# A graph network's second pass: twelve products done during the neighbour search, rows weighed in batches, norm products on four row groups

## The chip, the cores and the metric

The kernel runs on one core of one Trainium2 chip. The metric is device time in microseconds of one execution; the number compared is the median of several. Engines: PE (TensorE; PEld is its weight load), DVE (VectorE), ACT (ScalarE), POOL (GpSimd), SP (SyncE, which issues most DMAs).

## The reference, cut to what matters

Four graph layers over 2708 nodes with 128 features and a dense 2708 x 2708 matrix `adj`. The change lies in layer 0:

```python
def _lap_mul(A, x):
    d = 1.0 / jnp.sqrt(jnp.sum(A, axis=-1))
    return d[:, None] * (A @ (d[:, None] * x))
z = _lap_mul(A, x) @ W1 + b1
z = jax.nn.leaky_relu(z, negative_slope=0.1)
sq = jnp.sum(z * z, axis=-1)
d2 = jnp.maximum(sq[:, None] + sq[None, :] - 2.0 * (z @ z.T), 0.0)
S = jnp.exp(-jnp.sqrt(d2 + 1e-10) / 2.0)
S = jnp.where(ranks < 4, S, 0.0)        # the four nearest rows alone
A2 = S + A
out = _lap_mul(A2, x) @ W2 + b2
x = _layernorm(x + out)
```

Layers 1 to 3 (an attention layer and two more products with `adj`) follow; their code is the same before and after.

## The kernel before, in words

The nodes are 22 tiles of 128 rows, `t` = 0 to 21; the last has 20 rows (`FULL` = 21). The columns are C = 6 chunks of 512, 512, 512, 512, 384 and 276. `adj` is used transposed. Its row tiles 0 to 15 (`S` = 16) are streamed as panels of four tiles by one chunk (1 MB for a chunk of 512) through a ring of four slots; tiles 16 to 21 lie in SBUF for good (`res`).

**First pass** (lines 425 to 540): `adj` times y, then z for each tile, its transpose `zT`, and the norms. `turn_norms` writes `nsq3`, 3 rows of bf16 parts of the negated norms, on partitions 0 to 2.

**Search** (lines 623 to 651): for each tile, in the order 4 to 15, 0 to 3, 16 to 21 (n counts them from 0): ACT makes `z2` = 2 z (line 626); PE does six norm products `ones3` by `nsq3` (line 632, three rows deep, bf16) and six products `z2` by `zT` (line 642, f32) into the same six banks; ACT copies the six banks into one of three `key` buffers (line 643); DVE takes the eight largest (`max`, line 644, into `near`) and where they stand (`max_index`, line 645, into `where`).

**Weighing** (`weigh`, lines 586 to 617): for a range of tiles, the values in `near` become the weights `sim` of the four nearest, the new degrees `d2inv`, and the scaled rows `y2` = x times d2inv, which POOL multiplies and stores to DRAM (`y2_rows`); `others` sets a tile's own row apart. It is called three times: tiles 0 to 16 after t = 16, tiles 17 to 19 after t = 19, and 20, 21 at the end. The small arithmetic is DVE's, with Ln and Exp on ACT.

**Second pass** (`by_panels` at line 869): `adj` times `y2`, chunk by chunk, 22 products a chunk into one bank (acc pool of three). The 20-row products of three chunks go together, on three groups of 32 rows (`few`, line 96). Chunk 0 takes its tiles in the order 0 to 11, 16 to 19, 12 to 15, 20, 21. `ready` are the four panels of chunk 0, loaded before the search.

**Work hung on ticks** (`Due`, line 31): in the second pass PE, DVE and ACT run in the order written. Each product is a tick (132 in all), and `at(n, f)` puts work f behind tick n. `sum_near(t)`, at tick `near_at[t]` = 24 + 4.6 t, gathers three near rows of y2 for each row of the tile (POOL, line 672) and adds them up on DVE (line 685). `end_pass2(c)` sets out a chunk's end: `finish` (add_near on PE, the copy into hT on ACT, line 832) at n, no earlier than three ticks behind its last sum_near and 16 behind the chunk before; then norm0 at n + 2, turn at n + 9, find_c at n + 11, and for its tiles compare (DVE), times_w (PE, ACT), rank_rows (ACT) and rank_columns (PE) from n + 13 on. The last chunk's steps stand closer together (lines 851 to 866). `due.flush` runs what is left after the last product.

**PSUM** has eight banks: in the search six for `acc` and two for `mis`; in the pass three and three, one for `rk` and one for the places (`js_pool`, used after the pass).

Of the kernel before, what the change touches and what calls it, by code (L numbers as in the profile page):

```python
# [13 lines left out]
ALU = mybir.AluOpType  # L14
# [16 lines left out]
class Due:  # L31


    def __init__(self):
        self.n, self.work = 0, []

    def at(self, n, f, *args):
        self.work.append((n, len(self.work), f, args))
        self.work.sort(key=lambda w: w[:2])
# [13 lines left out]
def kernel(  # L53
# [54 lines left out]
    mis_pool = psum.enter_context(tc.tile_pool(name="mis", bufs=2, space=bass.MemoryType.PSUM))  # L108
# [80 lines left out]
    def by_panels(weights, done, tick=None, ready=(), first=None):  # L189

        ready = list(ready)
        accs = {}

        def product(c, i, src, w):
            lhsT = weights(i)[few(c) if i == FULL else slice(None)]
            start = c not in accs  # L200
            if start:
                accs[c] = acc_tile()
            stop = tick is None and i == (FULL if c % GROUPS == 0 else FULL - 1)
            nc.tensor.matmul(accs[c][: lhsT.shape[-1], :w], lhsT=lhsT, rhs=src, start=start, stop=stop)  # L204

        for c in range(C):
            w = cw[c]
            for i in [*(first if first and c == 0 else range(FULL)), *([FULL] if c % GROUPS == 0 else [])]:
                if i == FULL:
                    for n in range(c, c + GROUPS):  # L210
                        product(n, i, res[few(n), i - S, cols[n]], cw[n])
                    done(c, accs[c])
                    for _ in range(GROUPS if tick is not None else 0):
                        tick()
                    continue
                if i < S:
                    if i % 4 == 0:
                        if ready:
                            part = ready.pop(0)
                        else:  # L220
                            part = load_panel(i // 4, c)
                    src = part[:, i % 4, :w]
                else:
                    src = res[:, i - S, cols[c]]
                product(c, i, src, w)
                if i == FULL - 1 and c % GROUPS:
                    done(c, accs[c])
                if tick is not None:
                    tick()

# [133 lines left out]
    with tc.tile_pool(name="knn", bufs=1) as knn:  # L364
        nsq = knn.tile([P, T], F32, tag="nsq", name="nsq")
        nsq3 = knn.tile([3, N], BF16, tag="nsq3", name="nsq3")
        ones3 = knn.tile([3, P], BF16, tag="ones3", name="ones3")
# [47 lines left out]
        def turn_norms(c, ts, parts):  # L415
            ps = mis_tile()
            for t in ts:
                o = t * P - starts[c]
                nc.tensor.transpose(ps[:3, o : o + pw[t]], parts[: pw[t], t - ts[0], :], ident[: pw[t], : pw[t]])
            nc.scalar.copy(nsq3[:, cols[c]], ps[:3, : cw[c]])  # L420
# [165 lines left out]
        def weigh(ts):  # L586
# [4 lines left out]
            nc.vector.tensor_add(nr, nr, nsq[:, t0:t1, None].to_broadcast([P, t1 - t0, TOPK]))  # L591
            nc.vector.tensor_scalar(nr, nr, 0.0, DIST_EPS, op0=ALU.min, op1=ALU.subtract)
# [4 lines left out]
            nc.vector.tensor_reduce(dd, sm, AX.X, ALU.add)  # L597
            nc.vector.tensor_add(dd, dd, deg[:, t0:t1])  # L598
# [20 lines left out]
        ready = [load_panel(g, 0) for g in range(G)]  # L619
        tc.keep_in_program_order(nc.scalar.preload_act_table_set("natural_log_exp_and_others"))  # L620
        with tc.tile_pool(name="keys", bufs=3) as keys:

            for n, t in enumerate([*range(4, S), *range(4), *range(S, T)]):
                p = pw[t]
# [5 lines left out]
                def norms(c):  # L630
                    cs = cols[c]
                    nc.tensor.matmul(pks[c][:p, : cw[c]], lhsT=ones3[:, :p], rhs=nsq3[:, cs], start=True, stop=False)
# [5 lines left out]
                for c in range(C) if n else (5, 3, 2, 4, 1, 0):  # L638
                    if not n:
                        norms(c)  # L640
                    cs = cols[c]
                    nc.tensor.matmul(pks[c][:p, : cw[c]], lhsT=z2[:, :p], rhs=zT[:, cs], start=False, stop=True)  # L642
                    nc.scalar.copy(key[:p, cs], pks[c][:p, : cw[c]])  # L643
                nc.vector.max(near[:p, t, :], key[:p])  # L644
                nc.vector.max_index(where[:p, t, :], near[:p, t, :], key[:p])
                if t == T - 6:
                    weigh(range(0, T - 5))
                if t == T - 3:
                    weigh(range(T - 5, T - 2))
            weigh(range(T - 2, T))  # L650
# [5 lines left out]
    js_pool = psum.enter_context(tc.tile_pool(name="places", bufs=1, space=bass.MemoryType.PSUM))  # L656
# [161 lines left out]
    near_at = [24 + (23 * t) // 5 for t in range(T)]  # L818
# [49 lines left out]
    with tc.manual_schedule(engines={nc.tensor.engine, nc.vector.engine, nc.scalar.engine}):  # L868
        by_panels(
            rows_of(y2), end_pass2, due.tick, ready, [*range(S - 4), *range(S, T - 2), *range(S - 4, S), T - 2]  # L870
        )
        due.flush()
    late.close()
    more = ExitStack()
# [744 lines left out]
```

## Time and profile before

| | us |
|---|---|
| five runs | 1095.9, 1098.95, 1093.81, 1090.37, 1093.31 |
| their median | 1093.81 |
| the profiled execution: its time | 1099.03 |
| the profiled execution: its span | 1097.3 |
| mean granted PE clock in it | 0.966 |
| PE busy in the span | 999.9 (91%) |
| DVE / ACT / POOL busy | 643.0 / 338.9 / 266.2 |

Times in the trace count from the span's start. The first pass ends at about 157 us, the search runs to 302, the second pass from 295 to 443, the ranking to about 540, the attention layer's blocks to 760, and two more passes and the last layer to the end. A line of a timeline gives the start, the length, the engine, the source line, the operation, out<-in, and how many were merged; what stands in brackets is the idle time before it and what ended that. A matmul of f32 shows as two records.

### The profile page before, as it was taken

The page shows a single profiled execution, that of the slowest core. Times are in us where ns is not written, and L with a number is a line of the kernel's source. Part 1 is how long each engine was busy: PE and PEld are TensorE (multiplying, and loading weights), DVE is VectorE, ACT ScalarE, POOL GpSimd, SP SyncE. Part 2 cuts the span into 40 slices and gives each one's busy share as a digit, 9 for nine tenths or more (in the row PEclk, how much of TensorE's full clock was granted, in tenths as well). Part 3 has the DMA queues.
Part 4 walks back from the last instruction along what each step waited for, and adds up shares of the span by engine and source line. Part 5 has one row for each costly group of instructions (what it writes and reads, how often), then busy time and mean ns, then how long its engine had stood idle before and what let it go on. Part 6 is the DMA issues. An engine that isn't in the chain of part 4 may idle for free.

```text
span 1097.3 us, 11424 instructions
## 1 busy us (share of the span) xinstructions
PE 999.9 (91%) x3678; PEld 482.3 (44%) x3678; DVE 643.0 (59%) x1351; ACT 338.9 (31%) x614; POOL 266.2 (24%) x332
## 2 busy tenths in 40 slices
PE   0798999999995988698799999999999999999996
PEld 0345544444442556443233333334444644564444
DVE  5884448999942658763398999998112112132122
ACT  0000125555400234602466777665001100011000
POOL 4000000000564554106485444441112100000000
PEclk9989999999997999699899999999999999999998
DMA  9999330000283747398445545555674865574752
GB/s 341 362 320 276 115 120 1 0 1 1 61 283 92 229 133 215 131 326 267 126 131 160 143 134 152 148 150 188 208 252 140 280 223 187 172 238 156 243 159 75
DMA packets 109363, 190.30 MB, mean 173 GB/s; under 512 B 13650, under 2 KB 46690, under 8 KB 109294
## 3 DMA queue, kind: packets, MB, share of 16 engines
q1 hardware_dynamic: 91408, 151.79, 42.7%
q0 software_dynamic: 17712, 37.62, 12.4%
q8 instruction: 31, 0.51, 0.2%
q14 instruction: 38, 0.31, 0.1%
q10 hardware_dynamic: 174, 0.08, 0.0%
HBM read 214.37 MB, written 4.16 MB: 199 GB/s over the span
## 4 chain that ended last, share of the span: by engine, by line
PE 47%; DMA 1%; issue 1%; DVE 1%; POOL 0%; ACT 0%; SPq 0%; POOLq 0%; DVEq 0%
PE acc L204 27%; PE hacc L1280 9%; PE num L1423 9%; PE mis L285 1%; DMA ring<-in_adjT,slot_i 0%; PE mis L1554 0%; DMA ring<-carry 0%; ACT gb L234 0%; PE mis L1520 0%; PE mis L1550 0%; POOL ring L1301 0%; SPq L1438 0%; POOL rstd L253 0%; PE mis L1508 0%; POOL xws L890 0%
## 5 line engine op out<-in xcount | busy, mean ns | idle before, releaser
L1301 POOL DMA_INDIRECT ring<-in_adjT,slot_i x88 | 99.0, 1125 | 115.1 <-PE num L1423 88.0
L1423 PE MATMUL num<-ring,lw 128*64 128x512 f32 (+1 forms) x528 | 116.1, 561 | 3.1 <-DVE err L1265 1.3
L1280 PE MATMUL hacc<-inv,xws 128*128 128x512 f32 (+1 forms) x264 | 111.7, 559 | 0.4 <-issue 0.4
L642 PE MATMUL acc<-zT,z 128*128 128x512 f32 (+4 forms) x264 | 108.6, 558 | 0.0
L1255 ACT ACTIVATE inv<-num,plain 128x1024 f32<-128x1024 f32 x88 | 80.5, 915 | 61.4 <-PE num L1423 53.1
L253 POOL TENSOR_TENSOR rstd<-rstd,minus_half 128x4 f32<-128x4 f32 (+1 forms) x19 | 18.2, 956 | 315.0 <-DVE rstd L252 315.0
L643 ACT COPY key<-acc 128x512 f32<-128x512 f32 (+3 forms) x132 | 70.1, 534 | 59.9 <-issue 29.8
L234 ACT COPY gb<-acc 128x512 f32<-128x512 f32 (+2 forms) x18 | 9.6, 534 | 251.1 <-PE acc L204 251.1
L1265 DVE TENSOR_TENSOR err<-inv,num 128x1024 f32<-128x1024 f32 x88 | 74.3, 853 | 20.3 <-ACT inv L1258 18.6
L204 PE MATMUL acc<-ring,y 128*128 128x512 f32 (+2 forms) x192 | 81.1, 551 | 0.5 <-POOL sim L579 0.5
L1280 PEld LDWEIGHTS hacc<-inv,xws 128*128 128x128 f32 x264 | 46.5, 189 | 77.4 <-issue 48.1
L672 POOL DMA_INDIRECT got<-y_rows,where x66 | 69.8, 1058 | 43.1 <-DVE near_sum L685 22.7
L204 PE MATMUL acc<-ring,xs 128*128 128x512 f32 (+2 forms) x192 | 77.9, 549 | 0.0
L1272 DVE SCALAR_TENSOR_TENSOR inv<-gb,g_inv,inv 128x1024 f32<-128x1024 f32 x88 | 77.0, 912 | 0.1
L204 PE MATMUL acc<-ring,carry 128*128 128x512 f32 (+2 forms) x192 | 74.5, 542 | 0.0
L204 PE MATMUL acc<-ring,m_rows 128*128 128x512 f32 (+2 forms) x192 | 74.3, 542 | 0.0
L1269 DVE SCALAR_TENSOR_TENSOR inv<-err,inv 128x1024 f32<-128x1024 f32 x88 | 72.6, 863 | 0.1
L642 PEld LDWEIGHTS acc<-zT,z 128*128 128x128 f32 (+1 forms) x264 | 47.5, 188 | 55.0 <-issue 49.6
L1258 ACT ACTIVATE inv<-inv 128x1024 f32<-128x1024 f32 x88 | 67.6, 768 | 2.8
L644 DVE MAX8 near<-key 128x8 f32<-128x2708 f32 (+1 forms) x22 | 65.5, 2979 | 4.9 <-ACT key L643 4.9
L570 POOL TENSOR_TENSOR slot_e<-near,sim 128x44 f32<-128x44 f32 (+2 forms) x3 | 0.7, 241 | 271.8 <-DVE d2inv L598 267.7
L1423 PEld LDWEIGHTS num<-ring,lw 128*64 128x64 f32 x528 | 37.1, 139 | 64.4 <-issue 45.6
(327 smaller groups left out, 1376.6 us busy)
## 6 DMA issues: line engine op xcount, KB each, us to landing
ring<-in_adjT SPq DMA_DIRECT2D x86, 1024.0 KB
ring<-in_adjT SPq DMA_DIRECT2D x19, 768.0 KB
part<-in_adjT SPq DMA_DIRECT2D x12, 1024.0 KB
ring<-in_adjT SPq DMA_DIRECT2D x19, 552.0 KB
res<-in_adjT SPq DMA_DIRECT2D x4, 1280.0 KB
more<-in_adjT SPq DMA_DIRECT2D x4, 1024.0 KB
part<-in_adjT SPq DMA_DIRECT2D x3, 768.0 KB
part<-in_adjT SPq DMA_DIRECT2D x3, 552.0 KB
```

Of the source, the lines that this page charges most:

```text
L204: nc.tensor.matmul(accs[c][: lhsT.shape[-1], :w], lhsT=lhsT, rhs=src, start=start, stop=stop)
L642: nc.tensor.matmul(pks[c][:p, : cw[c]], lhsT=z2[:, :p], rhs=zT[:, cs], start=False, stop=True)
L643: nc.scalar.copy(key[:p, cs], pks[c][:p, : cw[c]])
L672: nc.gpsimd.indirect_dma_start(out=got[:p, :], out_offset=None, in_=y2_rows[:, :], in_offset=bass.IndirectOffsetOnAxis(ap=where[:p, t, k : ...
L1255: nc.scalar.activation(inv, num[:, :w], AF.Ln, scale=plain[:, 0:1], bias=plain[:, 1:2])
L1258: nc.scalar.activation(inv, inv, AF.Exp, scale=-1.0)
L1265: nc.vector.tensor_mul(err, inv, num[:, :w])
L1269: nc.vector.scalar_tensor_tensor(inv, err, 2.0, inv, op0=ALU.subtract, op1=ALU.mult)
L1272: nc.vector.scalar_tensor_tensor(inv, gb[:, col : col + w], g_inv[:, q : q + 1], inv, op0=ALU.max, op1=ALU.mult)
L1280: nc.tensor.matmul(haccs[:, o:e], lhsT=xws[:, q, :], rhs=inv[:, o:e], start=(q == 0), stop=(q == NQ - 1))
L1301: nc.gpsimd.indirect_dma_start(out=rows[i][:KC, n, :], out_offset=None, in_=adj_half[:, :], in_offset=bass.IndirectOffsetOnAxis(ap=slot_i[ ...
L1423: nc.tensor.matmul(num[n * (BJ + 2) : (n + 1) * (BJ + 2), o:e], lhsT=lw[:, 2 * q + n, :], rhs=rows[i][:, n, c0 + o : c0 + e], start=True, ...
```

## The change

It does these things:

- The last norms in hand, three DMAs on SP copy the rows 0 to 2 of `nsq3` to partitions 32, 64 and 96 (`NORMS` = 4). From the second tile of the search on, the norm product of chunk c reads row group c % 4. `ones3` and `nsq3` are made that tall.
- The two `mis` banks are given back before the search, and one bank, `acc0`, is taken for chunk 0 of the second pass.
- The four panels of chunk 0 are loaded behind those copies, in the order 1, 2, 3, 0. From the seventh to the eighteenth tile of the search (n = 6 to 17) PE also does the product of chunk 0 with tile n - 2 (4 to 15) into `acc0`. When a panel's fourth product has been put in, the first, second and third panel of chunk 1 are loaded in its place.
- PE's order in the search is the order written, from the second tile on.
- `weigh` is called for tiles 4 to 7, 8 to 11, 12 to 15 and 0 to 3, each after the last tile of the four, with its arithmetic on POOL (the sum over four weights as four additions); then for 16 to 19 after t = 19 and for 20, 21 at the end, on DVE as before.
- The second pass begins with chunk 0's tiles 0 to 3 and 16 to 19, then chunk 1's 0 to 3, then chunk 0's 20 and the 20-row products, then the rest of chunk 1; the other chunks as before. That makes 120 ticks. `near_at[t]` = 23 + 4.2 t. `by_panels` takes the order and the bank begun as arguments.
- The places' bank is taken after the pass, when `acc0` has been given back. `Due` numbers its entries by a counter of all that were put in (before, by the length of the list at that time).

```diff
-    def by_panels(weights, done, tick=None, ready=(), first=None):
+    def by_panels(weights, done, tick=None, ready=(), order=None, begun=None):
...
-        accs = {}
+        accs = dict(begun or {})
+        started = set(accs)
...
+        if order is None:
+            order = [(c, i) for c in range(C) for i in [*range(FULL), *([FULL] if c % GROUPS == 0 else [])]]
+        for c, i in order:
...
-            nc.scalar.copy(nsq3[:, cols[c]], ps[:3, : cw[c]])
+            nc.scalar.copy(nsq3[:3, cols[c]], ps[:3, : cw[c]])
...
-        def weigh(ts):
+        def weigh(ts, engine):
...
-            nc.vector.tensor_add(nr, nr, nsq[:, t0:t1, None].to_broadcast([P, t1 - t0, TOPK]))
-            nc.vector.tensor_scalar(nr, nr, 0.0, DIST_EPS, op0=ALU.min, op1=ALU.subtract)
+            engine.tensor_add(nr, nr, nsq[:, t0:t1, None].to_broadcast([P, t1 - t0, TOPK]))
+            engine.tensor_scalar(nr, nr, 0.0, DIST_EPS, op0=ALU.min, op1=ALU.subtract)
...
-            nc.vector.tensor_reduce(dd, sm, AX.X, ALU.add)
-            nc.vector.tensor_add(dd, dd, deg[:, t0:t1])
+            if engine is nc.vector:
+                nc.vector.tensor_reduce(dd, sm, AX.X, ALU.add)
+                nc.vector.tensor_add(dd, dd, deg[:, t0:t1])
+            else:
+                engine.tensor_add(dd, sm[:, :, 0], deg[:, t0:t1])
+                for k in range(1, TOPK):
+                    engine.tensor_add(dd, dd, sm[:, :, k])
...
-        ready = [load_panel(g, 0) for g in range(G)]
+        mis_psum.close()
...
+        acc0 = first_pool.tile([P, CW], F32, tag="first", name="acc0")
+        for g in range(1, NORMS):
+            nc.sync.dma_start(nsq3[32 * g : 32 * g + 3, :], nsq3[:3, :])
+        AHEAD = range(4, S)
+        panels0 = {g: load_panel(g, 0) for g in (*range(1, G), 0)}
+        ready = [panels0[0]]
+        batches = {7: range(4, 8), 11: range(8, 12), 15: range(12, 16), 3: range(4), T - 3: range(S, T - 2)}
...
+                if n == 1:
+                    search.enter_context(tc.manual_schedule(engines={nc.tensor.engine}))
...
-                    cs = cols[c]
-                    nc.tensor.matmul(pks[c][:p, : cw[c]], lhsT=ones3[:, :p], rhs=nsq3[:, cs], start=True, stop=False)
+                    r = slice(32 * (c % NORMS), 32 * (c % NORMS) + 3) if n else slice(3)
+                    nc.tensor.matmul(
+                        pks[c][:p, : cw[c]], lhsT=ones3[r, :p], rhs=nsq3[r, cols[c]], start=True, stop=False
+                    )
...
+                i = n - 2
+                if i in AHEAD:
+                    nc.tensor.matmul(
+                        acc0[:, : cw[0]], lhsT=y2[:, i, :], rhs=panels0[i // 4][:, i % 4, : cw[0]],
+                        start=(i == AHEAD[0]), stop=False,
+                    )
+                    if i % 4 == 3:
+                        ready.append(load_panel(len(ready) - 1, 1))
...
-                if t == T - 6:
-                    weigh(range(0, T - 5))
-                if t == T - 3:
-                    weigh(range(T - 5, T - 2))
-            weigh(range(T - 2, T))
+                if t in batches:
+                    weigh(batches[t], nc.gpsimd if t < T - 3 else nc.vector)
+            weigh(range(T - 2, T), nc.vector)
...
-    near_at = [24 + (23 * t) // 5 for t in range(T)]
+    near_at = [23 + (21 * t) // 5 for t in range(T)]
...
-        by_panels(
-            rows_of(y2), end_pass2, due.tick, ready, [*range(S - 4), *range(S, T - 2), *range(S - 4, S), T - 2]
-        )
+        tail = [FULL - 1, FULL]
+        order = [*((0, i) for i in (*range(4), *range(S, FULL - 1))), *((1, i) for i in range(4))]
+        order += [*((0, i) for i in tail), *((1, i) for i in range(4, FULL))]
+        order += [(c, i) for c in range(2, C) for i in [*range(FULL), *([FULL] if c % GROUPS == 0 else [])]]
+        by_panels(rows_of(y2), end_pass2, due.tick, ready, order, {0: acc0})
```

## The prediction

> **What bounds the kernel now.** I read the page's slices first: the search (157 to 302 us) and the second pass (295 to 443 us) are the only stages that the change touches. The table by stretches then gives, for each, its length, the busy time of PE, PEld, DVE, ACT and POOL, the granted clock, the DMA share and GB/s.
>
> ```profile
> 157.00:295.00 138.00, 136.84 (x413) 59.67 (x412) 129.46 (x100) 77.70 (x162) 13.30 (x47) 0.99 0.03 9
> 295.00:330.00 35.00, 34.94 (x90) 15.74 (x91) 18.05 (x48) 2.74 (x14) 20.99 (x37) 1.00 0.75 248
> 331.10:343.65 12.55, 0.00 (x0) 0.00 (x0) 0.70 (x2) 0.61 (x2) 6.99 (x8) 0.69 0.42 126
> 343.65:349.50 5.85, 5.84 (x13) 3.56 (x14) 3.25 (x16) 1.46 (x2) 0.00 (x0) 0.50 0.00 0
> ```
>
> In the search PE and DVE are both full; ACT is at 56%, POOL at 10%, the DMA queues nearly idle. The pass is PE's, but for one hole of 12.55 us, after which PE runs at half clock for 5.85 us. The timeline of one tile of the search shows both loops (start, length, engine, line, work):
>
> ```profile
> 240.71 1.31 PE L632 MATMUL acc<-nsq,ones 3*128 3x512 bf16 x6
> ...
> 241.95 4.81 PE L642 MATMUL acc<-zT,z 128*128 128x512 f32 x12
> ...
> 245.69 1.50 ACT L643 COPY key<-acc 128x512 f32<-128x512 f32 x3 [0.27 <-PE acc L642]
> 246.69 1.31 PE L632 MATMUL acc<-nsq,ones 3*128 3x512 bf16 x6
> ...
> 247.22 2.98 DVE L644 MAX8 near<-key 128x8 f32<-128x2708 f32 x1
> ```
>
> PE needs 1.24 us (240.71 to 241.95) for the six norm products and 4.74 for the six products: 5.98 a tile. DVE begins 0.03 us after the last key copy (245.69 + 1.50 = 247.19), so PE leads the loop; but DVE alone needs 5.97 (its MAX8 of two later tiles start at 283.83 and 289.80, with the keys lying ready). Shortening PE alone therefore gains 0.01 us a tile: about 0.3 us over 21 tiles. The end of the search and the start of the pass:
>
> ```profile
> 295.06 10.54 PE L204 MATMUL acc<-ring,y 128*128 128x512 f32 x24 [0.51 <-POOL sim L579]
> ...
> 301.82 0.17 DVE L598 TENSOR_TENSOR d2inv<-d2inv,deg 128x3 f32<-128x3 f32 x1
> ...
> 302.54 0.82 POOL L602 TENSOR_TENSOR y<-xs,d2inv 128x384 f32<-128x384 f32 x1
> ...
> 308.87 3.60 PE L204 MATMUL acc<-ring,y 128*128 128x512 f32 x8
> ...
> 312.30 2.08 PE L204 MATMUL acc<-res,y 128*128 128x512 f32 x8
> ```
>
> A product of the pass over 512 columns takes two passes of the array, 0.86 us in all (308.87 to 312.30 holds four). PE begins the pass while DVE still has 7 us of search to do, and the y2 of tiles 17 to 19 is only there at 303.36.
>
> **Norm products on four row groups.** The trace has no 3-row products on different groups. No overlap is the upper bound, 1.24 us a tile. The lower bound is four at once and then two: (512 + 384) of 2708 columns, 0.41 us. The nearest row is the last above: 312.30 to 314.32 holds one whole product (0.86) and three 20-row products on three row groups, so those took 1.16 where they would take 2.57 in a row, 0.45 of it. I take 0.45 × 1.24 = 0.56. In a tile without an added product the last norm must also wait for ACT's last copy, 0.50 us after the norms begin, so 0.75 there. PE then needs 4.74 + 0.75 = 5.5 us a tile without an added product and 4.74 + 0.56 + 0.86 = 6.16 with one.
>
> The Trainium skill (TensorEngine Tiling (Array Packing), Key Properties) speaks for the overlap, since tiles of the array run in parallel, and also against it: a change of the tiling mode drains the engine. Full fourfold packing would make the norms 0.31 us; a drain is in no row by itself.
>
> **Twelve products in the search.** 12 × 0.86 = 10.3 us leave the pass. Over tiles 2 to 17 (four without, twelve with) PE needs 4 × 5.5 + 12 × 6.16 = 95.9 us, DVE 16 × 5.97 = 95.5. So PE has no room left: DVE starves by about 0.4 us. The bounds are 0 (norms at 0.41) and 10.5 (norms at 1.24). The y2 that a product needs comes of a tile two or three before it, some 10 us against a weighing of some 6 (six POOL and five ACT operations of 0.2, a product of 1.09, key copies between); I charge nothing there.
>
> **The copies of the norms.** Three new DMAs on SP wait for the last norm cast (L420 ends at 165.77) and stand ahead of the four panel loads, which SP issued by 153.0. The panels are first read at tile 6 (about 203 us); 4 MB at the 276 GB/s seen below take 15 us, so they land by about 185: free. But the norms of tile 1, at 167.18 now, wait for the copies. A gather issued at 309.09 released DVE at 313.29, 4.2 us later; zero is the other bound. With an issue of 0.4 each I take 2 us of delay on PE, 0.75 of it won back in the shorter norms: 1.4 us later (0 to 3). Cover is gone here, since DVE idles at that point already.
>
> **Weighing in batches.** DVE loses four small operations and gets two comparisons: 2 × 0.17 = 0.3 us won. POOL gets four batches of six operations of 0.2 us and a product of 0.82 × 4/3 = 1.09, besides stores at 0.9 each, in a search where it is busy 13.3 of 138 us. ACT gets five short operations and a copy a batch, 4 × 1.2 = 4.8 us, beside 77.7 of 138. If ACT waits in line for POOL, the key copies are queued behind it, then PE's banks; two waits a batch of 1 us would be 8 us, and DVE's further keys cover it at first. I take 0.
>
> **Resuming the pass.** The search ends 1.4 − 0.3 − 0.3 + 0.4 = 1.2 us later. DVE's small operations still fall between its long ones, so y2 of 16 to 19 is ready at 303.36 + 1.2 + 0.27 (four tiles for three) = 304.9. PE has done its search by about 295, the four products 0 to 3 by 298.4, and then has nothing: idle for 6.5 us. At 304.9 it has 16 products of chunk 0 behind it; now it has (304.9 − 295.06)/0.86 = 11.4. So the twelve are worth 4.6 × 0.86 = 3.9 us, not 10.3: the rest fills time in which PE then waits.
>
> **The clock.** After the hole of 12.55 us the half clock lasted 5.85 us of work and cost 2.9. I charge 2.6 here; 0 to 3.4. The skill (TensorE: Matmul & The Clock Gate, Part 1) has an idle window of about 3.4 us halve the clock and a busy one restore it. It speaks against this change as the row does; by its one window the cost would be 1.7.
>
> **The tail.** Chunk 4's finding of c, rank and comparisons hang on ticks (one tick a product), and sixteen ticks lie between two chunks' ends. There are 120 ticks where there were 132, so find_c of chunk 4 falls at tick 116 of 120, not 123 of 132: its work is no longer covered.
>
> ```profile
> 435.37 0.91 PE L744 MATMUL mis<-xT,w_c 128*128 128x384 f32 x2 [0.92 <-ACT xT L739]
> ...
> 443.34 0.40 ACT L832 COPY hT<-acc 128x276 f32<-128x276 f32 x1
> ...
> 444.86 0.85 DVE L725 SCALAR_TENSOR_TENSOR xs<-mis,d2inv,xs 128x128 f32<-128x128 f32 x3 [2.51 <-PE mis L720]
> ```
>
> Now the last norm starts 9.5 us after that find_c, and 2.9 after the last product (442.0). With five fewer products between, the three comparisons of chunk 4 (1.6 us each behind 0.9 and a copy) still end 7.0 after find_c, now 3.5 after the last product; ACT's two sums of 2.1 to 2.5 us, queued before the last turn, make it about 1.9 us later (0 to 4).
>
> The gathers start when the last y2 row has landed (first at 309.09), 1.3 us each: tile t is there at about 309.1 + 3.9(t + 1) + 3. Chunk 0 is finished at tick 38, about 335, and needs tile 3 (328): covered, as all later chunks are by more. The bank of the places moves under acc0's, free a hundred us before its use: nothing.
>
> **Sum.** Pass −3.9 (search delay inside), clock +2.6, tail +1.9: **+0.6 us**, no change that can be told. The profiled execution took 1099.03 us (span 1097.3), 5.22 above the median of 1093.81; so 1099.6 in its terms and **1094.4** in the median's. With all bounds low, 3.9 + 1.2 better, 1088.7; the likeliest case's own range is 1089 to 1099.
>
> **Rivals.** *PE becomes the bound of the search (slower).* One mechanism: the norms don't overlap as the 20-row products do. Beyond 0.53 us for the six in a tile with a product, each tenth costs 1.2 us; at 1.24 it is 10.5 less the 0.4 counted. The idle time before the pass then shrinks, and with it the half clock (−2.6): 1094.4 + 10.1 − 2.6 = **1102**. For it: PE has no room at all in my own sum. Against: the 312.30 row.
>
> *The hole goes (faster).* No record says what held PE for 12.55 us; ACT's copy of chunk 0 waited, and the DMA share before it was 0.81 at 276 GB/s. Three panels of chunk 1 (3 MB of the 7.2 in that stretch) are now loaded in the search, where the share is 0.03. If that pressure makes the hole, 12.55 + 2.9 = 15.5 us go at most. The runs spread over 8.6 us and the profiled one is 5.2 above the median, so I count half: 7.7 better, **1086.7**. Against: nothing names DMA as the releaser.
>
> *All twelve pay:* 1093.81 − 10.3 = **1083.5**. It needs y2 of 16 to 19 seven us earlier, or other work for PE; DVE's order speaks against it.
>
> **Chances.** No change 0.42, PE bound 0.27, the hole goes 0.26, all twelve pay 0.05. What a measurement of this kernel can tell from no change is about 0.5%, 5.5 us. So faster 0.31, same 0.42, slower 0.27. The range 1084 to 1103 leaves out about 0.15: most of the last case, and the PE case with ACT's 8 us on top.
>
> **What would show it.** Right: search tiles 5.97 us apart by MAX8, an idle PE of 5 to 9 us before the products of 16, then a granted clock of 0.5, and the pass about as long to its end. Wrong: tiles 6.2 us or more apart in the twelve; norms over 0.6; no hole after chunk 0's finish; PE busy through 300 us.

## The result, and the profile after

| | kernel before | with the change |
|---|---|---|
| median, us | 1095.92 (79 runs, 1089.70 to 1102.27) | 1099.73 (42 runs, 1094.47 to 1106.91) |
| ratio, 95% interval | | 1.0035 (1.0024 to 1.0046) |
| profiled execution: time, span, granted clock | 1099.03, 1097.3, 0.966 | 1100.68, 1099.0, 0.956 |

The change costs 3.8 us (2.6 to 5.0). The prediction said +0.6 against the kernel before, "no change that can be told": inside its range, and inside 0.5%, but not by the sum it gave. Later runs found chips of another kind. On three of them the kernel before took 1062 to 1063.5 us, and on the one where the change itself was measured it cost 7.2 (4.1 to 10.2; the two intervals overlap). Below, chips on which the kernel before takes some 1096 us are the first kind, those with some 1062 the second.

The table by stretches of the changed kernel (length, busy time of PE, PEld, DVE, ACT and POOL, granted clock, DMA share, GB/s), with the search, the idle stretch before tile 16's product, the work behind it, the hole behind chunk 0's finish, and the work behind that:

```profile
157.00:304.00 147.00, 143.34 (x447) 60.46 (x445) 130.68 (x100) 79.94 (x183) 25.35 (x104) 0.97 0.10 33
304.57:311.22 6.65, 0.00 (x0) 0.00 (x1) 6.05 (x11) 1.04 (x6) 4.22 (x20) 0.89 0.49 158
311.22:316.50 5.28, 5.28 (x6) 2.19 (x7) 5.09 (x20) 1.00 (x4) 1.77 (x2) 0.50 0.24 67
344.59:350.36 5.77, 0.00 (x0) 0.00 (x1) 0.00 (x0) 0.62 (x2) 2.01 (x2) 0.73 0.15 34
350.36:354.10 3.74, 3.74 (x11) 2.71 (x12) 1.59 (x7) 1.25 (x1) 0.00 (x0) 0.50 0.87 280
```

The idle stretch of 6.65 us is new; half clock follows it (0.50). The hole of 12.56 us behind chunk 0's finish has become 5.77. The search, here counted to 304, ends some 7 us later (the last tile's MAX8 starts at 303.36, before at 295.83), and the next fences show where.

The timeline of a search tile with one of the twelve products:

```profile
254.10 0.55 PE L652 MATMUL acc<-nsq,ones 3*128 3x512 bf16 x6
...
254.57 4.81 PE L664 MATMUL acc<-zT,z 128*128 128x512 f32 x12
...
259.22 1.02 PE L668 MATMUL acc<-ring,y 128*128 128x512 f32 x2
...
260.65 1.55 PE L664 MATMUL acc<-zT,z 128*128 128x512 f32 x3
```

The six norms take 0.47 us (254.10 to 254.57) where they took 1.24; the tile takes PE 6.08 (254.57 to 260.65), against 5.97 for DVE.

Where DVE lost time. First, the second tile of the search:

```profile
167.51 1.35 SPq L633 DMA_DIRECT2D nsq<-nsq  x2
...
169.06 0.37 PE L652 MATMUL acc<-nsq,ones 3*128 3x512 bf16 x1 [0.65 <-DMA nsq<-nsq]
...
169.83 1.22 PE L652 MATMUL acc<-nsq,ones 3*128 3x512 bf16 x4 [0.40 <-DMA nsq<-nsq]
...
170.98 7.58 PE L664 MATMUL acc<-zT,z 128*128 128x512 f32 x12
...
179.02 2.98 DVE L674 MAX8 near<-key 128x8 f32<-128x2708 f32 x1 [4.21 <-ACT key L665]
```

PE waits for the copies of the norms (0.65, 0.40). Its twelve matmul records then take 7.58 us, not 4.8, because the granted clock is 0.5 from 169.8 to 176.6 (3.4 us of half clock at this spot in the kernel before, 6.8 here). DVE waits 4.21 us where it waited 1.42: the start costs 2.8.

Second, the weighing of a batch, here the first:

```profile
197.10 0.21 POOL L593 TENSOR_TENSOR near<-near,nsq 128x16 f32<-128x16 f32 x1 [183.69 <-DVE where L675]
...
197.75 0.21 ACT L595 ACTIVATE sim<-near 128x16 f32<-128x16 f32 x1 [2.08 <-POOL near L594]
...
199.62 0.20 ACT L606 ACTIVATE d2inv<-d2inv 128x4 f32<-128x4 f32 x1 [1.16 <-POOL d2inv L605]
199.73 0.57 ACT L665 COPY key<-acc 128x512 f32<-128x512 f32 x1
...
200.45 2.40 PE L652 MATMUL acc<-nsq,ones 3*128 3x512 bf16 x6
...
202.78 6.51 PE L664 MATMUL acc<-zT,z 128*128 128x512 f32 x12
...
209.74 2.98 DVE L674 MAX8 near<-key 128x8 f32<-128x2708 f32 x1 [0.80 <-ACT key L665]
```

ACT stands in line for POOL's sums (2.08, then 1.16 us), and POOL's first operation waits for DVE's FIND_INDEX8 of the tile. The key copies come behind. PE's norms wait for the banks (2.40 us instead of 0.47), the half clock follows (203.9 to 207.3), and after two more tiles DVE is idle for 0.80 us. The later batches cost 1.21 each, and there the step is direct. Here is the second:

```profile
222.57 0.22 ACT L595 ACTIVATE sim<-near 128x16 f32<-128x16 f32 x1 [1.08 <-POOL near L594]
222.70 0.37 ACT L665 COPY key<-acc 128x276 f32<-128x276 f32 x1
...
223.10 2.98 DVE L674 MAX8 near<-key 128x8 f32<-128x2708 f32 x1 [1.21 <-ACT key L665]
```

The last key copy of a tile stands behind the operation with which ACT waits for POOL, and DVE waits for that copy. Over the whole search DVE waits 12.1 us for keys in six places, where it waited 4.9 in two.

Third, the y2 of tiles 16 to 19, weighed on DVE:

```profile
300.20 0.16 DVE L593 TENSOR_TENSOR near<-near,nsq 128x16 f32<-128x16 f32 x1
...
303.29 0.15 DVE L594 TENSOR_SCALAR near<-near 128x16 f32<-128x16 f32 x1
...
306.25 0.14 DVE L600 TENSOR_REDUCE d2inv<-sim 128x4 f32<-128x16 f32 x1
...
309.36 0.13 DVE L601 TENSOR_TENSOR d2inv<-d2inv,deg 128x4 f32<-128x4 f32 x1
...
310.13 1.04 POOL L609 TENSOR_TENSOR y<-xs,d2inv 128x512 f32<-128x512 f32 x1
...
311.22 6.32 PE L206 MATMUL acc<-res,y 128*128 128x512 f32 x8 [6.65 <-POOL y L609]
```

Four operations of 0.15 us stand some 3 us apart, one between each two of DVE's long ones. The y2 is ready at 311.17, 7.8 us later than that of tiles 17 to 19 before (303.36).

What PE waited for from the pass to the end of the ranking, the longest entries, with the change:

```profile
PE mis L747 <- ACT hT L859: 13.0, 4, 5.8
PE acc L206 <- POOL y L609: 6.7, 1, 6.7
```

and in the kernel before:

```profile
PE mis L720 <- ACT hT L832: 13.6, 3, 12.6
PE mis L737 <- DVE xs L277: 3.7, 1, 3.7
...
PE mis L720 <- issue: 3.4, 1, 3.4
```

(line: total, times, longest). The waits behind the finishes (L747; L720 twice) fell from 17.0 to 13.0 us in total, and the wait of 6.7 for tile 16's y2 was added.

### The profile page after: what moved, and what is told of

The parts are those of the page before. It is cut to its first block, busy times and chain, and to the rows that moved or that the text cites. A ratio compares the mean times of both kernels' runs of the same rounds, so it can differ in the third digit from the quotient of the medians.

```text
span 1099.0 us, 11503 instructions
## 1 busy us (share of the span) xinstructions
PE 995.6 (91%) x3678; PEld 478.8 (44%) x3678; DVE 642.8 (58%) x1349; ACT 340.8 (31%) x631; POOL 278.1 (25%) x390
## 4 chain that ended last, share of the span: by engine, by line
PE 65%; DVE 16%; DMA 5%; another core or an unknown queue 5%; ACT 3%; issue 3%; POOL 1%; SPq 1%; ACTq 0%; POOLq 0%; DVEq 0%
PE acc L206 31%; PE num L1454 8%; PE hacc L1311 8%; PE acc L430 7%; DVE where L675 5%; DVE near L674 5%; DMA res<-in_adjT 3%; PE acc L664 2%; PE acc L1207 1%; DMA ring<-in_adjT,slot_i 1%; PE mis L286 1%; DMA part<-in_adjT 1%; DVE mask L806 1%; DVE both L485 1%
## 5 line engine op out<-in xcount | busy, mean ns | idle before, releaser
L1332 POOL DMA_INDIRECT ring<-in_adjT,slot_i x88 | 96.4, 1096 | 116.3 <-PE num L1454 88.6
L664 PE MATMUL acc<-zT,z 128*128 128x512 f32 (+4 forms) x264 | 111.3, 570 | 0.0
L1296 DVE TENSOR_TENSOR err<-inv,num 128x1024 f32<-128x1024 f32 x88 | 74.3, 853 | 20.4 <-ACT inv L1289 19.7
L674 DVE MAX8 near<-key 128x8 f32<-128x2708 f32 (+1 forms) x22 | 65.3, 2969 | 12.1 <-ACT key L665 12.1
L206 PE MATMUL acc<-ring,y 128*128 128x512 f32 (+2 forms) x168 | 72.0, 557 | 0.0
L675 DVE FIND_INDEX8 where<-near,key 128x8 uint32<-128x2708 f32 (+1 forms) x22 | 65.4, 2972 | 0.0
```

Of the source, the lines that this page charges most:

```text
L1296: nc.vector.tensor_mul(err, inv, num[:, :w])
L1332: nc.gpsimd.indirect_dma_start(out=rows[i][:KC, n, :], out_offset=None, in_=adj_half[:, :], in_offset=bass.IndirectOffsetOnAxis(ap=slot_i[ ...
```

## The experiments

Twelve runs were made, in four jobs. Each ratio is to the kernel before on the same chip. In the first job (experiments 1 to 4) that took 1097.26 us (1096.96 without one run of 5782.09), in the others 1062.11, 1063.23 and 1063.47: the first kind, then the second. The change itself did not run in the first job. What is said there of a time against the change compares ratios, with 1.0035 for the change; the intervals of experiments 1 and 3 overlap with its own.

**1. Row groups from the third tile on**

```diff
-                    r = slice(32 * (c % NORMS), 32 * (c % NORMS) + 3) if n else slice(3)
+                    r = slice(32 * (c % NORMS), 32 * (c % NORMS) + 3) if n > 1 else slice(3)
```

> The second tile of the search also reads its norms from row group 0, so that only the third tile on needs the copies. Theory (the start of the search waits for the copies, and the half clock that follows stretches the second tile): the MAX8 of the second tile falls from 179.0 back to about 176.2 us, the half clock of 169.8 to 176.6 shrinks to the 3.4 us of before, and the search and the whole end 2 to 3 us sooner than with the change as it is. Rival (DVE is the bound and its later keys cover the start): that MAX8 is sooner, but the end of the search and the time stay within 1 us.

Ratio 1.0051 (1.0025 to 1.0077). The time was not shortened by anything that this interval tells. The trace shows the piece itself, in the group of all MAX8 (count, busy, mean, idle before them):

```profile
L674 DVE MAX8 near<-key 128x8 f32<-128x2708 f32 x21 | 62.4, 2969 | 9.3 <-ACT key L665 9.3
```

DVE's idle time falls from 12.1 to 9.3: the 2.8 us of the start are real. The product of tile 16 starts 4.8 us sooner (306.44; 1.95 of that was there at the first MAX8 already), the last ranking product 1.9 sooner (460.34 for 462.24). The profiled execution took 2.4 us less than the change's, but the median ratio of its 12 runs did not fall. What is won ahead of the pass is not simply won at the end.

**2. All norms on one row group, without the copies**

```diff
-        for g in range(1, NORMS):
-            nc.sync.dma_start(nsq3[32 * g : 32 * g + 3, :], nsq3[:3, :])
...
-                    r = slice(32 * (c % NORMS), 32 * (c % NORMS) + 3) if n else slice(3)
+                    r = slice(3)
```

> All norm products on row group 0, without the three copies; the twelve products stay in the search. Theory (row groups are what makes room for the twelve): six norms take 1.24 us instead of 0.47 to 0.55, a tile with a product needs 6.85 us of PE against 5.97 of DVE, so the search ends 12 x 0.8 = 9.6 less about 3 (the start no longer waits) = 6 to 7 us later; of that up to 6.65 us is taken back by the idle time before the product of tile 16 only if the y2 of 16 to 19 did not hang on the search, which it does, so the time is 4 to 9 us longer than with the change. Rival (the delays of the search come from ACT in line behind POOL and cover this): within 1.5 us of the change.

Ratio 1.0094 (1.0060 to 1.0128), some 6 us over the change by the ratios. The theory's sign and size hold for the time, but its path is not the one written down:

```profile
L672 DVE MAX8 near<-key 128x8 f32<-128x2708 f32 x21 | 62.6, 2982 | 14.2 <-ACT key L663 14.2
```

DVE is idle for 14.2 us, only 2.1 more than with row groups. The start is as before (1.42), and the longer norms cover the waits for POOL's sums, which I had added up as if they came on top. The last MAX8 comes 2.6 us later than in the change; the rest of the 6 us came in the pass and behind it. So the row groups are worth about 5 us of search when the start is left out, and 2 with it.

**3. Chunk 1's tiles 0 to 7 ahead of chunk 0's tiles 16 to 20**

```diff
-        order = [*((0, i) for i in (*range(4), *range(S, FULL - 1))), *((1, i) for i in range(4))]
-        order += [*((0, i) for i in tail), *((1, i) for i in range(4, FULL))]
+        order = [*((0, i) for i in range(4)), *((1, i) for i in range(8)), *((0, i) for i in range(S, FULL - 1))]
+        order += [*((0, i) for i in tail), *((1, i) for i in range(8, FULL))]
```

> The order of the pass alone: chunk 0 tiles 0 to 3, then chunk 1 tiles 0 to 7, then chunk 0 tiles 16 to 20 and the 20-row products, then the rest of chunk 1. Four products of 0.86 us fill the idle 6.65 us before the product of tile 16, leaving about 3.2. Theory (the idle time is on the path, with the half clock behind it): 3.4 us gained, and up to 2.6 more if what is left of the idle time no longer halves the clock. Rival (the pass is held by the gathers and the hole behind chunk 0's finish, which only starts sooner): the hole grows by what is won, and the time stays within 1 us of the change.

Ratio 1.0069 (1.0039 to 1.0098): not shorter, and if anything longer. The idle stretch before tile 16 is gone, with its half clock, and comes back behind the finish:

```profile
338.12 0.80 PE L719 MATMUL acc<-ident,near_sum 128*128 128x128 f32 x2 [5.15 <-DVE near_sum L712]
...
352.76 1.12 DVE L752 SCALAR_TENSOR_TENSOR xs<-mis,d2inv,xs 128x128 f32<-128x128 f32 x4 [12.43 <-remote]
...
356.58 1.25 PE L764 MATMUL mis<-ident,xs 128*128 128x128 f32 x4 [6.69 <-DVE xs L278]
```

PE now waits 5.15 us for tile 3's gathered rows and 6.69 for chunk 0's normalized rows. That is what the rival foretold: PE's early work only makes it arrive earlier at a wait that hangs on the gathers.

**4. Each batch weighed, and each product done, one tile later**

```diff
-        batches = {7: range(4, 8), 11: range(8, 12), 15: range(12, 16), 3: range(4), T - 3: range(S, T - 2)}
+        batches = {8: range(4, 8), 12: range(8, 12), 0: range(12, 16), 16: range(4), T - 3: range(S, T - 2)}
...
-                i = n - 2
+                i = n - 3
```

> Each batch of the search is weighed one tile later, and each of the twelve products is done one tile later. Theory (ACT stands in line behind POOL's sums of a batch, the key copies behind ACT, and DVE starves): POOL's first two operations of a batch then run ahead of ACT, the waits of 2.1 and 1.1 us at the weighing lines of ACT fall to under 0.3 for the first, the idle time of DVE before the eight largest by key copies falls from 12.1 us to 8 or less, and the time is 3 to 4 us shorter than with the change. Rival (PE alone needs more than DVE in a tile with a product, 6.07 against 5.97, and the start took the rest): within 1 us of the change.

Ratio 1.0087 (1.0056 to 1.0117), some 6 us over the change by the ratios. The mechanism of this edit fell too: ACT's wait for POOL at its first weighing line is still 5.5 us in all (5.8 in the change), POOL's first operation still starts right behind a FIND_INDEX8, and DVE's idle time fell by 1.2 only:

```profile
L674 DVE MAX8 near<-key 128x8 f32<-128x2708 f32 x21 | 62.3, 2967 | 10.9 <-ACT key L665 10.9
...
L595 ACT ACTIVATE sim<-near 128x16 f32<-128x16 f32 x5 | 1.1, 216 | 7.0 <-POOL near L594 5.5 <-DVE near L594 1.5
```

The y2 of tile 16 came 2.0 us sooner, and the pass still ended later, with three idle stretches of PE behind finishes (7.10, 4.39 and 4.64 us) where the change has two.

**What these four share.** Two of them shortened the search and one filled PE's idle time, and none was faster. In the changed kernel's timeline, behind chunk 0's finish:

```profile
341.82 1.05 PE L719 MATMUL acc<-ident,near_sum 128*128 128x128 f32 x8
...
346.13 1.01 POOL L699 DMA_INDIRECT got<-y_rows,where  x1 [0.30 <-issue]
349.72 0.59 ACT L859 COPY hT<-acc 128x512 f32<-128x512 f32 x1 [36.61 <-remote]
...
350.36 2.08 PE L747 MATMUL mis<-w,hT 128*128 128x128 f32 x8 [5.77 <-ACT hT L859]
```

PE's last sum into chunk 0 is recorded as done at 342.87, but ACT, which waits for nothing else, copies at 349.72. In the trace PE's six semaphore updates that belong to the matmuls of 340.5 to 342.9 are all found between 349.49 and 349.70, 0.04 us apart. At this point POOL has issued 24 gathers in an unbroken row (15 that DVE has used up, and nine buffers), the last at 346.13. The copy, or in experiment 3 the next step, DVE's norm, follows the first gather by some 34 us in every kernel traced on the first kind, whatever PE did before:

| kernel | first gather, us | chunk 0 goes on, us | difference |
|---|---|---|---|
| before | 309.09 | 343.02 | 33.9 |
| the change | 315.53 | 349.72 | 34.2 |
| 1, groups from the third tile | 310.74 | 345.15 | 34.4 |
| 2, one group | 318.02 | 352.62 | 34.6 |
| 3, other order (DVE's norm) | 318.71 | 352.76 | 34.1 |
| 4, weighed later | 313.55 | 348.10 | 34.6 |

So on this kind of chip the time at which the pass goes on follows the gathers, and not PE's work. Whether it follows their start or the end of the row this table can't tell, since every row has 24. My next theory was that PE's signals are held back while gathers are issued, so that fewer buffers make the row, and the hole, shorter.

**5 to 7. Fewer buffers for gathered rows**

```diff
-    got_pool = late.enter_context(tc.tile_pool(name="got", bufs=9, side="right"))
+    got_pool = late.enter_context(tc.tile_pool(name="got", bufs=6, side="right"))
```

and the same with 4 in the changed kernel and in the kernel before.

> The change with six buffers for gathered rows instead of nine; nothing else. Theory (while POOL issues gathers one behind the other, PE's semaphore signals are held back until about 2.4 us after the last of them; the unbroken row after the first y2 is 15 gathers that DVE uses up plus as many as there are buffers, so 24, each 1.3 us): the row is 21 long and ends 3.9 us sooner, ACT's copy of chunk 0 comes 30.3 us after the first gather and not 34.2, the idle PE behind chunk 0's finish falls from 5.77 to about 1.9 us, and that behind chunk 1's (row of 12, then 9) from 4.78 to about 1; with the half clock behind each, 5 to 12 us shorter than the change. Rival 1 (panel loads or DMA traffic hold PE): the holes stay where they are, the time within 2 us. Rival 2 (fewer buffers starve DVE's sums, which then hold the finishes): longer by several us.

> The change with four buffers for gathered rows. Theory: the first row is 19 gathers long and ends 6.5 us sooner than with nine, before PE's own work for chunk 0 is done, so no idle PE is left there nor behind chunk 1; gain as with six buffers and up to 3 us more. Rival 1 (traffic holds PE): no effect. Rival 2 (a gather takes 4.2 us from issue to use, so four buffers give one gather in 1.1 us at best, and each wait of DVE for PE stops the row): the later chunks' sums come late, the pass ends several us later than with six.

> The kernel before the change with four buffers for gathered rows instead of nine. Theory: ACT's copy of chunk 0 comes 6.5 us sooner (336.5 instead of 343.0), the hole shrinks from 12.56 to about 6 us, and some of the half clock behind it goes: 5 to 8 us shorter than before, ratio 0.993 to 0.995. If the change is then still compared four buffers against four, it should be 0 to 4 us faster, since its own twelve products now lie on the path. Rival (traffic holds PE): ratio 1.000.

Ratios 1.0113 (1.0085 to 1.0141), 1.0196 (1.0162 to 1.0229) and, for the kernel before with four, 1.0077 (1.0050 to 1.0104). All longer: the rival of starving. DVE's waits for gathered rows in the pass (total, times, longest), with six buffers:

```profile
DVE near_sum L712 <- DMA got<-y_rows,where: 27.2, 15, 3.9
```

and with four:

```profile
DVE near_sum L712 <- DMA got<-y_rows,where: 46.1, 20, 4.7
```

With nine, on a chip of the second kind, they are 19.7 us in ten places. These runs do not tell the theory apart, though. This job ran where the kernel before took 1062.11 us, and in none of its traces did a signal come late: there was no hole to shrink.

**8. Three edits joined**: four buffers, the edit of 1 and the order of 3.

> The change with four buffers, row groups from the third tile on, and the order with eight of chunk 1's products ahead of chunk 0's tiles 16 to 20. Theory (each of the three shortens its own piece once the gathers no longer hold PE's signals): the start of the search 2.8 us sooner, the idle time before tile 16's product 6.65 down to about 3, and no hole behind chunk 0: 3 to 6 us shorter than the change with four buffers alone, and under the time before. Rival (the pass then waits for the first gathers instead, which start about 316 us and hold tile 3's sum to about 332): no shorter than four buffers alone but for the 2.8.

Ratio 1.0150 (1.0114 to 1.0186): 4.9 us under four buffers alone by the ratios, which is within the theory's 3 to 6, though too wide an interval to shut out the rival's 2.8. That it would come under the kernel before was wrong by 16 us. PE waits 2.48 and 2.51 us for gathered rows at chunk 0's sums, as the rival has it.

**9 to 11. The change again, and six buffers, beside each other**

> The change as it is, on the chip of this job. The four kernels with four and six buffers ran on a chip where the kernel before took 1062 us; none of their matmul signals came late and no idle PE stood behind the finishes, so that they can't be set against the change's 1.0035, which was measured where the kernel before took 1096. Theory (the loss of the change is the later search, some 7 us; where PE's signals are held back during the gathers, a smaller hole behind chunk 0 gives back part of it, elsewhere nothing does): on a chip with 1062, ratio 1.007 to 1.012; on a chip with 1096, 1.002 to 1.005 again. Rival (the later search is hidden everywhere, the 1.0035 is the half clock): 1.002 to 1.005 on both.

> The change with six buffers for gathered rows, beside the change with nine on the same chip. Theory (held-back signals while gathers are issued, on chips of the 1096 kind): there ACT's copy of chunk 0 comes about 30.3 us after the first gather instead of 34.2, the idle PE behind it falls from 5.8 to about 2 us, and the time is 4 to 10 us under that with nine. On a chip of the 1062 kind no signal is late, and six buffers are 0 to 4 us slower than nine. Rival (traffic of the panels holds PE): on a chip of the 1096 kind the idle time stays at 5 us or more, and the time too.

> The kernel before with six buffers instead of nine. Theory: on a chip of the 1096 kind the hole of 12.56 us behind chunk 0 shrinks by 3.9 us and the smaller one behind chunk 2 too, ratio 0.992 to 0.997, which would be under both kernels; on a chip of the 1062 kind there is no hole to shrink, and the ratio is 1.000 to 1.005. Rival: 1.000 to 1.005 on both.

This job's chip was of the second kind again (1063.23). The change: 1.0068 (1.0039 to 1.0096), 7.2 us longer, at the edge of the theory's 1.007 to 1.012; the interval reaches the rival's 1.002 to 1.005 too. With six buffers: 1.0102 (1.0073 to 1.0130), 5.3 us over nine, a little more than the 0 to 4 expected. The kernel before with six: 1.0005 (0.9984 to 1.0026), no difference, so that its trace can stand for the kernel before on such a chip. The change's own trace there, behind chunk 0's finish:

```profile
340.80 1.05 PE L719 MATMUL acc<-ident,near_sum 128*128 128x128 f32 x8
...
341.88 0.59 ACT L859 COPY hT<-acc 128x512 f32<-128x512 f32 x1 [29.74 <-PE acc L719]
...
342.46 1.00 POOL L699 DMA_INDIRECT got<-y_rows,where  x1 [0.30 <-issue]
...
343.40 1.05 PE L747 MATMUL mis<-w,hT 128*128 128x128 f32 x8
```

Same program, same row of 24 gathers (314.58 to 345.08), and ACT copies 0.03 us after PE's sum while POOL goes on issuing. There is no hole. So the gathers alone do not hold PE's signals; it takes something else that differs between chips, and that stays open. The traces of the first kind also lack some of these signals: 879 stand in the change's for 902 matmuls that send one, and 23 to 55 are missing in each of the six, none in the eight of the second kind. So the recording may have been disturbed there as well as the signals, and no run here separates the two. Whether a shorter row shortens the hole on a chip that has it was not measured.

What the change loses there instead, near the end of the pass:

```profile
416.23 0.35 DVE L712 SCALAR_TENSOR_TENSOR near_sum<-got,sim,near_sum 128x128 f32<-128x128 f32 x1 [2.51 <-DMA got<-y_rows,where]
...
421.37 0.56 PE L824 MATMUL rk<-ones_b,mask 128*128 128x1 bf16 x15 [4.92 <-DVE mask L806]
```

DVE waits for a gathered row, then has a norm and a comparison to do, and PE, whose ranking product is next in the written order, is idle for 4.92 us (2.12 at the same place in the kernel before with six buffers).

**12. Tiles 16 to 19 weighed on POOL, and the edit of 1**

```diff
-                    weigh(batches[t], nc.gpsimd if t < T - 3 else nc.vector)
+                    weigh(batches[t], nc.gpsimd)
```

> The change with row groups from the third tile on, and with tiles 16 to 19 weighed on POOL as the other batches are, so that their four small operations no longer stand between DVE's last MAX8 and FIND_INDEX8 (in the change they start at 299.25, 302.34, 305.29 and 308.40 us). Theory (the start costs 2.8; the idle 6.65 before tile 16's product and the half clock of 2.65 behind it are on the path): the y2 of 16 to 19 is ready about 8 us sooner, PE has no idle stretch before tile 16's product, and on a chip of the 1062 kind, where no signal is held back, the time is 8 to 12 us under the change's there, ratio 0.996 to 1.001. On a chip of the 1096 kind the end of the first row of 24 gathers still sets when PE goes on behind chunk 0 (34.2 us after the first gather), the idle time only moves there, and the ratio is 0.999 to 1.004. Rival (the gathers, which start with the y2 of tiles 20 and 21, hold chunk 0's finish or the tail): no more than the 2.8 of the start is won on either.

Ratio 1.0025 (1.0007 to 1.0042): the best of the changed kernels, about 4.6 us under the change on such chips by the ratios, and still not under the kernel before. Theory and rival each have half:

```profile
297.70 1.04 POOL L609 TENSOR_TENSOR y<-xs,d2inv 128x512 f32<-128x512 f32 x1 [0.89 <-ACT d2inv L607]
...
301.30 3.60 PE L206 MATMUL acc<-res,y 128*128 128x512 f32 x8
...
316.15 1.17 POOL L699 DMA_INDIRECT got<-y_rows,where  x1 [9.41 <-DMA y_rows<-y]
...
335.67 0.80 PE L719 MATMUL acc<-ident,near_sum 128*128 128x128 f32 x2 [4.86 <-DVE near_sum L712]
```

The y2 of 16 to 19 is made from 297.70 on, and tile 16's product runs at 301.30 without a wait; the 6.6 us are gone. But the first gather starts at 316.15 (314.58 in the change on such a chip), 6.3 us after the last store of y2 was issued (2.4 in the change). Between the two the DMA engines' share was 0.57 against 0.36, with more panel loads ahead; that the loads held the store is not shown. PE waits 4.86 us for tile 3's sum instead, and the clock is at half from 332.8 to 339.6.

## Why the prediction came out as it did

On the chips of the result "no change that can be told" was right and its size was off by 3.2 us (+3.8 for +0.6); on the second kind the change came out at 0.68% (0.39 to 0.96), more than the 0.5% that I had called no change. That it came out right is in part luck: a search that ends 6 us later than foreseen is partly made good by a shorter hole, which I had only as a rival. From PE's first product of the pass to the last ranking product, in the profiled executions:

| us | first kind: before, change | second kind: before with six buffers, change |
|---|---|---|
| PE begins the pass | 295.06, 300.87: +5.8 | 293.88, 299.92: +6.0 |
| twelve products of 0.86 | −10.3 | −10.3 |
| PE's waits in the pass and ranking | 28.3, 32.3: +4.0 | 11.5, 22.0: +10.5 |
| left over | +3.8 | +4.3 |
| last ranking product starts | 458.94, 462.24: +3.3 | 437.00, 447.51: +10.5 |

The waits are the sums of the whole view of which the longest entries stand above, less what lies outside the stretch, and of the same view on the second kind; the fourth row is what is left of the difference. It is the half clock: half of the time that PE was busy at a clock of 0.5 in these stretches is 7.1 and 11.4 us on the first kind, 4.2 and 8.2 on the second, so 4.3 and 4.0 more with the change. On the first kind 1.6 of the 3.3 us are made good behind this stretch in this pair of executions, which differ by 1.65 at the end; the medians differ by 3.8. On the second kind 4.9 of the 10.5 us come back before the attention blocks begin (504.00 and 509.58), a stretch in which the kernel before with six buffers has two more half-clock stretches, 3.4 and 6.8 us, and the change none.

- **Norms on row groups** (0.56, and 0.75 without a product): 0.47 and 0.75. Right, by the row of the 20-row products that it was taken from. The lower bound was 0.41, so changing the tiling can cost no more than 0.06 us a tile here.
- **A product of the pass** (0.86): right. The "two passes of the array" behind it are two records in the trace; what the array does in them no run shows.
- **PE against DVE in a tile with a product** (6.16 against 5.97): 6.08. Right.
- **The copies of the norms** (1.4 us, 0 to 3): 2.8. The wait was rightly placed. The half clock that stood behind a PE wait at this spot was not in the sum, though the trace of before had 3.4 us of it there.
- **ACT in line behind POOL** ("I take 0", bound 8): 4.4 us (0.80 and three times 1.21). **This is the step that failed.** I had written that DVE's further keys cover the wait. They cover it in part once, but PE had no room to win the lead back: with 6.08 against 5.97 a tile, a lost lead is never made good before the next batch. Those 0.11 a tile, some 0.4 a batch, are part of the 1.21. Experiment 1 took away the 2.8 and left these waits as they were; experiment 4 took away one of them. In experiment 2, where PE is slower still, ACT waits only 1.6 us for POOL at that line (5.8 in the change). No run took POOL's sums out of ACT's way, so this step is read from the trace.
- **The end of the search** (+1.2, y2 of 16 to 19 at 304.9): 311.2. The two steps above add up to 7.2, and 0.84 was there before the search. By 311.2 the kernel before has done (311.22 − 295.06)/0.86 = 18.8 products, so at that moment the change, with its 16, was 2.8 products, 2.4 us, behind, not 3.9 ahead. The hole and the half clock make up the rest of the account.
- **Idle PE, then half clock** (6.5 and 2.6): 6.65, and 5.28 us of work at half clock, 2.6. Right. The Trainium skill (TensorE: Matmul & The Clock Gate, Part 1) has one window of about 3.4 us bring the clock down or up; an estimate by it is 1.7. The records have 6.8 us at half clock here (309.7 to 316.5), so the row was the better guide.
- **The gathers are covered** ("all later chunks by more"): wrong. They start 6.4 us later (315.53 for 309.09), the ticks are closer together (4.2 for 4.6 a tile), and they end up on the path: in experiments 3, 8 and 12 at chunk 0, on the second kind of chip near the end. On the first kind no sum came late at chunk 0, but the hole there follows the gathers, as the table of the 34 us shows.
- **The tail** (+1.9, 0 to 4): the mechanism was right, the size a little small. From the end of the last product to the last turn it is 9.3 us (442.41 to 451.71) where it was 6.4 (442.14 to 448.52): +2.9. PE's idle stretches of over 0.3 us between 415 and 446 us are 2.14, 1.06, 2.46 and 1.35, together 7.0, against 0.70, 1.28, 0.92 and 0.35, together 3.25: +3.8, in part ahead of the last product, where the sum had nothing.
- **The rival that the hole goes** (0.26): half of it came. Idle PE behind the finishes fell from 12.56 + 3.38 to 5.77 + 4.78, 5.4 us. But the reason given, pressure of panel loads, has the table by stretches against it: the DMA share was 0.15 in the hole that was left. The time at which PE goes on moved with the gathers (+6.7 us), and PE arrived later at it. On the second kind there was no hole with the same loads.
- **The rival that PE bounds the search** (0.27) did not come in its form. Experiment 2 is that rival made real: 1.0094.
- **The signs.** An idle PE of 5 to 9 us and a clock of 0.5 behind it came true. Tiles 5.97 apart came true only between two waits: from the seventh tile's MAX8 to the eighteenth's (209.74 to 279.43) it is 6.3 us a tile on the mean, and "6.2 us or more apart in the twelve" was named as a sign of being wrong. This one did tell of the late search.

**The clock** as a whole. Mean span and granted clock of all runs give span × (1 − clock), what half clock can have cost at most, and the remainder:

| | span, us | clock | lost at most, us | remainder, us |
|---|---|---|---|---|
| before, first kind (29 runs) | 1095.9 | 0.9639 | 39.5 | 1056.4 |
| the change, first kind (44) | 1098.3 | 0.9572 | 47.0 | 1051.3 |
| before, second kind (18) | 1061.6 | 0.9752 | 26.3 | 1035.3 |
| the change, second kind (7) | 1068.3 | 0.9689 | 33.3 | 1035.0 |
| experiment 12 (12) | 1063.8 | 0.9689 | 33.1 | 1030.7 |

The 29 runs of the first row are those of the first job, the 44 of the second are those of the result. By this table the changed kernel gets its work into 5 us less on the first kind, and into the same on the second, and gives at most 7.0 to 7.5 us more to the clock on both. Half clock while PE is idle costs nothing, so this is an upper bound of the clock's share and not a proof that the clock alone decides. Still, it says where such an edit has to be judged: it moved work and left idle stretches of PE in several places, and the longer ones are paid for twice, as idle time and as half clock behind it.

No version was faster than the kernel before. The nearest were the kernel before with six buffers (1.0005) and experiment 12 (1.0025).

## What to carry to other kernels

When work is pulled into a stage that two engines already fill, a wait in an in-order queue is not covered by buffers: price each such wait in full unless the engine behind it has spare time to win its lead back. Before crediting an earlier start of the next stage, follow every chain that the stage feeds: here the gathers start with the last rows of the search, and on the first kind of chip the time at which the pass went on followed them and not PE's products. Charge each longer idle stretch of PE with half clock behind it: in these runs all of 3.3 to 12.6 us in the pass had it at their end or within 1.5 us, and some of 2.1 to 2.5 did too. Compare experiments only with a control on the same chip.

## What was not expected of the hardware

- **Two kinds of chip.** The same kernel takes 1096 us on some and 1062 to 1063.5 on others. On the first, PE's semaphore updates came up to 14 us after the matmul's recorded end while POOL issued a long row of gathers (343.00 for an end at 329.38 in the kernel before), the last of them some 3.6 to 4.1 us after the last gather of the row had started; on the others none was late with the same row. In the table of PE's waits the kernel before shows it as 28.3 us against 11.5 (with six buffers). What causes it was not found.
- **Six products of three rows on four row groups** take 0.47 us for 1.24, 0.38 of it.
- **One weighing of four tiles** took 11.0 us where its four small operations stood between DVE's long ones (300.20 to 311.17 in the change), and 4.4 us on POOL and ACT (294.38 to 298.74 in experiment 12).
